# Two of 39 expert tiles of a routed feed-forward layer move into a conditional block

## The chip, the cores and the metric

The kernel runs on one core of a Trainium2 chip. Its engines are TensorE (PE, with its weight loads shown apart as PEld), VectorE (DVE), ScalarE (ACT), GpSimd (POOL) and SyncE (SP), which issues most of the DMAs. Each engine runs its own stream of instructions in order, and streams wait for each other on semaphores. The metric is the time of one execution on the device, in microseconds.

## What is computed

The reference is one decoder layer in float32 over x of 8 sequences of 512 tokens with 256 features: windowed self-attention, cross-attention to 64 context rows, and a layer of its own with attention over the 8 sequences and a mixture of 8 experts. The change concerns the experts alone:

```python
xf = y.reshape(S * B, D)                 # 4096 rows of 256
idx = jnp.argmax(xf @ Wg.T, axis=-1)     # one of 8 experts a row
out = jnp.zeros_like(xf)
for e in range(E):
    m = (idx == e)[:, None]
    h = jax.nn.relu(xf @ W1[e] + b1[e])  # 256 -> 1024
    out = out + m * (h @ W2[e] + b2[e])  # 1024 -> 256
z = layer_norm(y + out, g2, be2)         # and x + z is the result
```

Each row needs its own expert only, so how many rows an expert has depends on the data.

## The kernel before

The kernel sends each row to its expert by sorting. The last layer runs over 8 blocks of 512 rows. When a block is normalised and its experts are known (`block_end`), four indirect DMAs from POOL scatter its rows into a table in memory, `rows_d`, in which each expert has a region of its own. A row of it is 513 words: the row for the matmul, the row of the residual stream, and the number of the token.

**Tiles.** Work on the experts is cut into tiles of 128 rows of a single expert. 4096 rows make 32 full tiles, and each of 8 experts may have a last tile that isn't full, so there are at most `NT` = (4096 + 8 x 127) // 128 = 39. The kernel runs all 39, whatever the counts are.

**Three tables** say which expert and which rows a tile has. The first is made when 4 blocks are known and has the 9 full tiles that must exist by then (`NT1`); the second after 6 blocks goes up to tile 17 (`NT2`); the third, after all 8, has the remaining 22. `table` compares counts with multiples of 128: `nt` holds the tiles of each expert, `first` the sum over the experts before it. A tile past the last one used still gets an expert number (the last one's) and rows past that expert's end. For rows past the end `void` is 1, and `FAR` is added to their index, so that the gather and the scatter leave them out.

**A tile** (`expert_tile`) goes in steps. A gather by POOL brings 128 rows (L1129). SP reads the expert's number from the table into a register (L1146) and loads W1 of that expert, 1 MB (L1149), b1 (L1151) and b2, spread over the partitions (L1156). PE transposes the rows (L1167), DVE copies them out (L1169). PE makes the 1024 hidden features as 16 products (L1178), ACT and DVE take half of the relus each (L1183, L1185), PE makes 8 products with W2, which lies on the chip for all experts (L1193). DVE adds the residual (L1200) and takes mean and variance (L1203, L1204, L1206), POOL raises to the power -0.5 (L1207), DVE scales (L1209, L1210), and POOL scatters the rows to the output (L1211). At L1188 and L1189 POOL adds residual and biases.

**Order.** `expert_tile` is a generator, and each `yield` ends a step. `in_steps` runs the generators of all tiles beside each other, one step of each at a time, with tile i begun i steps late. So the first product of tile i+1 stands between the two products of tile i, and the gathers and loads run ahead. `in_order` then ties PE, DVE, ACT and POOL to the order in which instructions were written; SP's stream is placed by the framework. Six buffers take the gathered rows in turn, four the output rows (`r`, one allocation for four tiles).

Of the kernel before, what the change touches and what calls it, by code (L numbers as in the profile page):

```python
# [8 lines left out]
F32 = mybir.dt.float32  # L9
I32 = mybir.dt.int32  # L10
BF16 = mybir.dt.bfloat16
AF = mybir.ActivationFunctionType
ALU = mybir.AluOpType
# [4 lines left out]
P = 128  # L18
# [5 lines left out]
E, DF = 8, 1024  # L24
# [7 lines left out]
NGRP = S // GP  # L32
NT = (B * S + E * (P - 1)) // P
NB1, NB2 = 4, 6
NT1, NT2 = (-(-(n * NG * P - E * (P - 1)) // P) for n in (NB1, NB2))
ROW = 2 * D + 1
FAR = 1 << 20
# [2 lines left out]
PREFIX, TURN, VALUES, SMALL, SCORES, OTHER, EXPS, LOADS = range(8)  # L40
# [9 lines left out]
@contextmanager  # L50
def in_order(tc):

    traced = tc.nc.cur_bb.bb.instructions
    before = len(traced)
    yield
    et = mybir.EngineType
    last = {et.PE: None, et.DVE: None, et.Activation: None, et.Pool: None}
    for i in list(traced)[before:]:
        if i.engine in last:
            if last[i.engine] is not None:  # L60
                tc.add_manual_dep(
                    i,
                    last[i.engine].name,
                    mybir.DependencyInfo(mybir.DependencyClass.NoSync, mybir.DependencyReason.DATA),
                    reason="in_order",
                )
            last[i.engine] = i


def in_steps(works):  # L70

    step = 0
    works = sorted(works, key=lambda w: w[0])
    active, begun = [], []
    while works or active:
        while works and works[0][0] <= step:
            w = works.pop(0)
            begun.insert(0, [w[2] if len(w) > 2 else OTHER, w[1]])  # L80
            active.insert(0, begun[0])
        todo = sorted(active, key=lambda w: w[0])
        active = []
        while todo:
            w = todo.pop(0)
            rank = next(w[1], StopIteration)
            if isinstance(rank, tuple):
                w[0] = rank[1]
                todo = sorted([w] + todo, key=lambda w: w[0])
            elif rank is not StopIteration:  # L90
                w[0] = OTHER if rank is None else rank
                active.append(w)
        order = {id(w): i for i, w in enumerate(begun)}
        active.sort(key=lambda w: order[id(w)])
        step += 1
# [3 lines left out]
def decoder_kernel(ctx: ExitStack, tc: tile.TileContext, a: dict, out: bass.AP):  # L99
    nc = tc.nc  # L100
# [9 lines left out]
    rows_d = dram.tile([E * B * S, ROW], I32, name="rows_d")  # L110


    group_rows = dram_disjoint_views(rows_d, NGRP + NT)
# [95 lines left out]
    new = {}  # L209
# [4 lines left out]
    if True:  # L214
        wp = p1.enter_context(tc.tile_pool(name="wp1", bufs=1))
# [510 lines left out]
    if True:  # L726
# [277 lines left out]
        scatters = []  # L1004

        def traced():
            return nc.cur_bb.bb.instructions

        known = (4 * NB1, 4 * NB2, 4 * NBLK)
# [75 lines left out]
        def counts():  # L1085
            ps = ps_m.tile([P, E], F32, tag="m")
            nc.tensor.matmul(ps, new["ones"], seens[-1], start=True, stop=True)
            return ps

        def make_table(name, n, whole):  # L1090

            wp, taken = new["w"], new["taken"]
            rest = wp.tile([P, E], F32, name=name + "rest")
            nc.vector.scalar_tensor_tensor(rest, taken, -float(P), counts(), ALU.mult, ALU.add)
            base = wp.tile([P, E], F32, name=name + "base")
            nc.vector.scalar_tensor_tensor(
                base, taken, float(P), cst[:, C_E4 : C_E4 + E], ALU.mult, ALU.add
            )
            if whole:
                nc.vector.tensor_scalar(rest, rest, float(1 - P), None, ALU.add)  # L1100
            first, nt = table(name, rest, ALU.is_gt, n, base, not whole)
            if whole:

                take = wp.tile([P, E], F32, name=name + "take")
                nc.vector.tensor_scalar(take, first, -1.0, float(n), ALU.mult, ALU.add)
                nc.vector.scalar_tensor_tensor(take, take, 0.0, nt, ALU.max, ALU.min)
                nc.vector.tensor_tensor(taken, taken, take, ALU.add)
            yield
# [3 lines left out]
        def expert_tile(i):  # L1112
# [3 lines left out]
            k = sum(i >= n for n in at) - 1  # L1116
            (eidx, srci, void), j = tables[k], i - at[k]
            if i < 6:
# [10 lines left out]
            nc.gpsimd.indirect_dma_start(  # L1129
                out=t.bitcast(I32),  # L1130
                out_offset=None,
                in_=group_rows[NGRP + i],
                in_offset=bass.IndirectOffsetOnAxis(ap=srci[:, j : j + 1], axis=0),
                bounds_check=E * B * S - 1,
                oob_is_err=False,
            )
            gather = traced()[-1]
            for scatter in scatters[: known[k]]:
                tc.add_manual_dep(
                    gather,  # L1140
                    scatter,
                    mybir.DependencyInfo(mybir.DependencyClass.Sync, mybir.DependencyReason.DATA),
                    reason="rows",
                )
# [5 lines left out]
            b1 = small.tile([P, NFC], F32, tag="b1", name=f"b1_{i}")  # L1150
            nc.sync.dma_start(b1, a["b1"][bass.ds(e_sp, 1)].rearrange("o p c -> p (o c)"))  # L1151

            if i % 4 == 0:
                new["r"] = qsh.tile([P, 4, D], F32, tag="qT", name=f"r_{i}")
            r = new["r"][:, i % 4]
            nc.sync.dma_start(r, a["b2"][bass.ds(e_sp, 1)].to_broadcast([P, D]))  # L1156
# [35 lines left out]
            for f in range(NFC):  # L1192
# [21 lines left out]
                in_=r,  # L1214
# [11 lines left out]
            works.append((F0 + 4 * n + 15, block_end(n, 0, NG)))  # L1226
        for k, (nb, n) in enumerate(((NB1, NT1), (NB2, NT2 - NT1), (NBLK, NT - NT2))):
            works.append((F0 + 4 * nb + 16, make_table(f"t{k}", n, nb < NBLK)))
        for i in range(NT):
            works.append((F0 + 4 * NB1 + 18 + i, expert_tile(i), VALUES))  # L1230
        with in_order(tc):
            in_steps(works)


def _constants():
# [40 lines left out]
def build(nc, arrays):  # L1276
    args = {
        name: nc.dram_tensor(f"in_{name}", v.shape, mybir.dt.from_np(v.dtype), kind="ExternalInput").ap()
        for name, v in arrays.items()
    }  # L1280
    out = nc.dram_tensor("out_0", (B, S, D), F32, kind="ExternalOutput").ap()
    with tile.TileContext(nc) as tc:
        decoder_kernel(tc, args, out)
# [52 lines left out]
```

## Time and profile before

| what | us |
|---|---|
| median of 3 runs (lowest, highest) | 1179.1 (1176.48, 1179.41) |
| profiled execution | 1174.85 |
| its span, first to last instruction | 1172.9 |
| 39 gathers of tiles, first and last issue | 841.2, 1129.1 |
| first and last scatter of rows to the output, issue | 880.6, 1162.0 |

The profile is of one execution. Its span is 1.95 us shorter than the time of that execution, and that lies 4.25 us under the median of the timed runs. All times within the trace count from the start of the span. Rows of the trace name an engine, a line of the kernel, the operation and the tiles; a "q" behind an engine's name means its sequencer, which waits, branches, loads registers and issues. The costliest groups of the expert part, as the page has them (line, engine, operation, out<-in, shapes, count, then busy us, mean ns of one, and idle time of the engine just before with what ended it):

```profile
L1178 PE MATMUL hps<-tT,w 128*128 128x128 f32 x1248 | 146.1, 275 | 0.4 <-issue 0.4
...
L1193 PE MATMUL ps<-w,h 128*128 x624 | 141.0, 379 | 0.0
...
L1207 POOL TENSOR_TENSOR rs<-rs,nhalf 128x1 f32<-128x1 f32 x39 | 22.9, 588 | 77.8 <-DVE rs L1206 65.6
```

The counts are those of 39 tiles: 32 and 16 matmul instructions of each, and one power.

### The profile page before, as it was taken

To read this page: it belongs to the slowest core of one execution; us is meant where nothing else is said; L and a number is where in the kernel's file an instruction comes from. 1 tells how busy PE (TensorE), PEld (TensorE's weight loads), DVE (VectorE), ACT (ScalarE), POOL (GpSimd) and SP (SyncE) were. 2 spreads that over 40 slices of the span, in tenths; PEclk is the share of its full clock that TensorE was granted. 3 is DMA by queue.
4 is the path that set the end of the run, shared out by engine and by line. 5 is a ranking of instruction groups with operands and counts; after the bars stand their busy time and mean duration, and the time that the engine had idled before them with its cause. 6 is when DMAs were issued, how large, how long until landed. Compare 5 with 4: busy or idle time off the path is not lost.

```text
span 1172.9 us, 24541 instructions
## 1 busy us (share of the span) xinstructions
PE 1087.1 (93%) x8960; PEld 791.9 (68%) x8960; DVE 721.2 (61%) x1833; ACT 584.4 (50%) x2047; POOL 499.7 (43%) x581
## 2 busy tenths in 40 slices
PE   6798999989989989999898899999799999999995
PEld 3555656656566565665555567666588999999994
DVE  2947758588485794866743535666656765555553
ACT  2876767668686686765942265555332111111110
POOL 2242623335323353153431333545555667555553
PEclk9997999999999999999989999999999999999998
DMA  6000001010010000100001670111445968666630
GB/s 208 11 1 1 11 1 46 2 37 11 2 46 3 19 28 1 42 6 28 29 1 40 185 226 1 37 69 42 137 142 200 296 219 260 207 206 207 209 110 7
DMA packets 60742, 97.65 MB, mean 83 GB/s; under 512 B 15946, under 2 KB 43981, under 8 KB 60624
## 3 DMA queue, kind: packets, MB, share of 16 engines
q1 hardware_dynamic: 53072, 75.08, 20.4%
q0 software_dynamic: 7552, 21.02, 5.3%
q8 instruction: 72, 1.18, 0.4%
q14 instruction: 46, 0.38, 0.1%
HBM read 81.12 MB, written 17.71 MB: 84 GB/s over the span
## 4 chain that ended last, share of the span: by engine, by line
PE 71%; DVE 15%; ACT 8%; DMA 2%; POOL 2%; issue 1%; SPq 0%; POOLq 0%; DVEq 0%
PE ps L186 12%; PE ps L191 12%; PE hps L1178 12%; PE ps L1193 11%; ACT s L464 5%; DVE nm L460 2%; PE sc L417 2%; DVE s L444 2%; PE ps L180 2%; PE av L523 2%; PE ps L857 2%; PE xav L659 2%; DVE kg L377 1%; PE av L894 1%; PE pt L494 1%; DVE nm L598 1%
## 5 line engine op out<-in xcount | busy, mean ns | idle before, releaser
L464 ACT ACTIVATE s<-s,nm 128x144 f32<-128x144 f32 (+1 forms) x512 | 203.4, 406 | 12.3 <-DVE nm L460 12.3
L1183 ACT ACTIVATE h<-hps,b 128x128 f32<-128x128 f32 x156 | 44.6, 368 | 220.6 <-issue 190.3
L1178 PE MATMUL hps<-tT,w 128*128 128x128 f32 x1248 | 146.1, 275 | 0.4 <-issue 0.4
L1178 PEld LDWEIGHTS hps<-tT,w 128*128 128x128 f32 x1248 | 142.8, 192 | 1.2 <-issue 0.6
L1193 PE MATMUL ps<-w,h 128*128 x624 | 141.0, 379 | 0.0
L500 POOL TENSOR_TENSOR pc<-pT,cst 128x512 f32<-128x512 f32 x96 | 123.1, 1303 | 27.1 <-DVE pT L496 26.7
L1193 PEld LDWEIGHTS ps<-w,h 128*128 128x128 f32 x624 | 115.7, 190 | 14.1
L464 ACT ACTIVATION_READ_ACCUMULATOR s<-s,nm 128x1 f32 x512 | 100.0, 195 | 0.0
L475 POOL COPY rx<-s 128x128 f32<-128x128 f32 x48 | 14.8, 308 | 190.6 <-ACT s L464 190.6
L460 DVE TENSOR_REDUCE nm<-s 128x8 f32<-128x1152 f32 (+1 forms) x64 | 84.5, 1320 | 13.2 <-POOL s L453 9.4
L1185 DVE TENSOR_SCALAR h<-hps,b 128x128 f32<-128x128 f32 x156 | 43.9, 344 | 75.0 <-ACT h L1183 60.9
L444 DVE COPY_PREDICATED s<-upto_q,sc 128x512 f32<-128x512 int32 x96 | 65.0, 731 | 24.6 <-ACT s L443 24.5
L417 PE MATMUL sc<-kz,qT 32*128 32x512 f32 (+1 forms) x512 | 76.4, 606 | 4.0 <-DVE s L436 3.1
L159 POOL TENSOR_TENSOR rs<-rs,nhalf 128x4 f32<-128x4 f32 (+1 forms) x33 | 33.8, 1024 | 108.2 <-DVE rs L158 108.0
L494 PE MATMUL pt<-cst,s 128*128 128x128 f32 x512 | 74.0, 285 | 2.5 <-ACT pT L498 1.0
L494 PEld LDWEIGHTS pt<-cst,s 128*128 128x128 f32 x512 | 61.3, 146 | 15.6 <-issue 7.2
L443 ACT COPY s<-sc 128x512 f32<-128x512 f32 x96 | 51.6, 590 | 35.6 <-PE sc L417 35.6
L478 DVE RECIPROCAL rc<-sm 128x8 f32<-128x8 f32 x64 | 12.6, 196 | 77.6 <-ACT s L464 77.6
L186 PE MATMUL ps<-fxT,w_fwqkv 128*128 128x512 f32 x128 | 58.8, 604 | 0.0
L186 PE MATMUL ps<-xT,w_wqkv 128*128 128x512 f32 x128 | 58.3, 598 | 0.0
L883 POOL TENSOR_TENSOR fs<-fs,sm 128x512 f32<-128x512 f32 x32 | 33.4, 1044 | 56.0 <-DVE sm L882 53.7
L1207 POOL TENSOR_TENSOR rs<-rs,nhalf 128x1 f32<-128x1 f32 x39 | 22.9, 588 | 77.8 <-DVE rs L1206 65.6
(240 smaller groups left out, 2309.4 us busy)
## 6 DMA issues: line engine op xcount, KB each, us to landing
w<-in_W SPq DMA_DIRECT2D x47, 1024.0 KB
r<-in_b SPq DMA_DIRECT2D x39, 128.0 KB
xb<-in_x SPq DMA_DIRECT2D x8, 512.0 KB
y<-x2d SPq DMA_DIRECT2D x32, 128.0 KB
x2d<-xb SPq DMA_DIRECT2D x7, 512.0 KB
mi<-in_mask SPq DMA_DIRECT2D x8, 128.0 KB
mj<-in_maskT SPq DMA_DIRECT2D x8, 128.0 KB
w_wqkv<-in_wqkv SPq DMA_DIRECT2D x1, 768.0 KB
```

The lines of the kernel that those rows point to most:

```text
L186: nc.tensor.matmul(ps, w[:, k, o0 : o0 + P], xT[:, k, :], start=k == 0, stop=k == 1)
L191: nc.tensor.matmul(ps, xT[:, k, t0 : t0 + P], w[:, k, o0 : o0 + D], start=k == 0, stop=k == 1)
L417: nc.tensor.matmul(ps[j // 2][:, j % 2].rearrange("p r w k -> p r (w k)"), qT[rows[j], hf, q0 : q0 + P], kz[rows[j], hf, :, q0 + P - nw * ...
L443: nc.scalar.copy(s4, ps[jj][:, :, :, 0, :])
L444: nc.vector.copy_predicated(s4, upto_q.unsqueeze(1).unsqueeze(1).to_broadcast([P, 2, 2, P]), ps[jj][:, :, :, 1, :],)
L460: nc.vector.tensor_reduce(nm, s[:, :, :nk], AX.X, ALU.max, negate=True)
L464: nc.scalar.activation(s[:, h, :nk], s[:, h, :nk], AF.Exp, bias=nm[:, h : h + 1], accum_out=sm[:, h : h + 1],)
L494: nc.tensor.transpose(pt[:, h, :], s[:, 4 * jj + h, :P], ident)
L500: nc.gpsimd.tensor_tensor(pc[:, hs, :], pT[:, hs, :], upto_k.unsqueeze(1).to_broadcast([P, 4, P]), ALU.mult,)
L1178: nc.tensor.matmul(ps[:, f, :], w1[:, k, f * P : (f + 1) * P], tT[:, k, :], start=k == 0, stop=k == 1)
L1183: nc.scalar.activation(h[:, f, :], ps[:, f, :], AF.Relu, bias=b1[:, f : f + 1])
L1193: nc.tensor.matmul(ps, h[:, f, :], new["w2"][:, bass.ds(e_pe, 1), f, :].rearrange("p o d -> p (o d)"), start=f == 0, stop=f == NFC - 1,)
```

## The change

A constant `NTC` = 37 is added, and the pipeline holds tiles 0 to 36. Tiles 37 and 38 are written behind it, in a block that all five engines enter or jump over by a number from memory. That number, `nt_i`, is made with the third table: the sum of `first` and `nt` of the last expert, so the number of tiles that the table uses, turned into an integer. The block is entered if it is over `NTC - NT2` = 20.

```diff
+NTC = 37
...
             first, nt = table(name, rest, ALU.is_gt, n, base, not whole)
+            if not whole:
+
+                nt_all = wp.tile([P, 1], F32, name="nt_all")
+                nc.vector.tensor_tensor(nt_all, first[:, E - 1 : E], nt[:, E - 1 : E], ALU.add)
+                new["nt"] = wp.tile([P, 1], I32, name="nt_i")
+                nc.vector.tensor_copy(new["nt"], nt_all)
...
-                in_=group_rows[NGRP + i],
+                in_=group_rows[NGRP + i] if i < NTC else rows_d,
...
-            for scatter in scatters[: known[k]]:
+            for scatter in scatters[: known[k]] if i < NTC else []:
...
-            if i % 4 == 0:
+            if i % 4 == 0 or i == NTC:
                 new["r"] = qsh.tile([P, 4, D], F32, tag="qT", name=f"r_{i}")
...
-        for i in range(NT):
+        for i in range(NTC):
             works.append((F0 + 4 * NB1 + 18 + i, expert_tile(i), VALUES))
         with in_order(tc):
             in_steps(works)
+
+        with tc.If(nc.values_load(new["nt"][0:1, 0:1], min_val=0, max_val=NT) > NTC - NT2):
+            in_steps([(i, expert_tile(i), VALUES) for i in range(NTC, NT)])
```

`values_load` puts the number into a register of each of the five engines, and each engine compares and branches for itself. In the program that is built from it each engine's stream has four parts behind the pipeline: the block, a part for the other case that brings the semaphores to the values that the block would have left (with an instruction on POOL for those of the indirect DMAs), a part in which the two meet again, and the end of the program. The last steps of tile 36 (L1207, L1209, L1210, L1211) stand in the part where the two meet. In front of the compare-and-branch DVE, ACT and POOL have six semaphore waits. In the block the gathers read `rows_d` as a whole and depend on all that was written to it, where those of the pipeline have views of it and named scatters to wait for. Tile 37 takes a new allocation of output rows.

## The prediction

> **What bounds the kernel now.** I read the page's first two parts, then a table by stretches of the last 320 us, then the chain of waits at its end. In the page:
>
> ```profile
> span 1172.9 us, 24541 instructions
> ...
> PE 1087.1 (93%) x8960; PEld 791.9 (68%) x8960; DVE 721.2 (61%) x1833; ACT 584.4 (50%) x2047; POOL 499.7 (43%) x581
> ...
> PE   6798999989989989999898899999799999999995
> PEclk9997999999999999999989999999999999999998
> ```
>
> The last ten slices of PE are full, at an undiminished clock. The stretches say it in numbers (length, then busy us and count of each engine, clock, DMA share, GB/s):
>
> ```profile
> core 0: us, PE busy (x) PEld busy (x) DVE busy (x) ACT busy (x) POOL busy (x), PEclk, DMA share, GB/s
> 1050.00:1100.00 50.00, 50.00 (x346) 46.76 (x345) 24.81 (x83) 8.01 (x28) 27.82 (x35) 1.00 0.65 212
> 1100.00:1150.00 50.00, 50.00 (x346) 46.81 (x345) 24.59 (x83) 8.01 (x28) 25.78 (x32) 1.00 0.40 123
> ```
>
> From 950 us to the last matmul PE never idles, DVE and POOL are half idle, DMA has room. So the expert tiles cost what their matmuls cost. The chain's last pieces (start, length, what):
>
> ```profile
> 1130.67 3.46 PE ps L1193 x16
> 1134.13 0.22 PE pt L1167 x2
> 1134.35 3.57 PE hps L1178 x32
> 1137.92 3.46 PE ps L1193 x16
> ...
> 1148.62 3.57 PE hps L1178 x32
> 1152.19 6.92 PE ps L1193 x32
> ...
> 1160.28 0.17 DVE rs L1206
> ...
> 1160.59 0.66 POOL rs L1207
> 1161.24 0.56 issue
> 1161.80 1.28 POOLq L1282
> ```
>
> One tile is 0.22 + 3.57 + 3.46 = 7.25 us of PE. The last product ends at 1159.12; behind it stand DVE's normalisation, the power on POOL, a last scatter, and the end of the program, which hangs on one row of POOL's queue:
>
> ```profile
> L1282 POOLq DRAIN  x3: 40/107/10337, 1161.8 to 1172.7; - x3
> ```
>
> POOL drains for 10.3 us (min/median/max in ns, so the 10337 is the one that starts at 1161.80), to 1172.14; the closing barriers follow.
>
> **Is the block skipped?** The condition is "tiles of the last table over 37 - 17 = 20". Counting the reference's own argmax on these inputs gives experts of 307, 294, 269, 642, 610, 1093, 688 and 193 rows: 3+3+3+6+5+9+6+2 = 37 tiles, 17 of them in the first two tables, so exactly 20. The trace agrees. Here are the moments at which the scatters of tiles 35 to 38 move data:
>
> ```profile
> 1145.90:1146.60 0.70, 0.70 (x5) 0.62 (x4) 0.17 (x1) 0.50 (x2) 0.70 (x2) 1.00 0.53 187
> 1153.10:1153.80 0.70, 0.70 (x5) 0.61 (x4) 0.34 (x2) 0.32 (x2) 0.70 (x2) 1.00 0.27 96
> 1160.10:1160.80 0.70, 0.00 (x0) 0.00 (x0) 0.67 (x3) 0.00 (x0) 0.21 (x1) 1.00 0.04 1
> 1163.50:1164.20 0.70, 0.00 (x0) 0.00 (x0) 0.00 (x0) 0.00 (x0) 0.00 (x0) 0.50 0.04 1
> ```
>
> 187 GB/s for a full tile, half of it for tile 36 (193 - 128 = 65 rows), nothing for tiles 37 and 38: all their rows lie past the bound. They cost PE time and yield nothing.
>
> **Removed.** Two tiles: on PE 2 x 7.25 = **14.50 us**, all on the path, since the stretch from 1144.62 to 1159.12 holds 14.48 us of PE work. With them go on SP two loads of W1 (1 MB each), of b1 and b2 and two index loads; on POOL two gathers, two scatters and six small operations; on DVE and ACT the relus and normalisation. None of it ended a wait of PE here, so it brings nothing more. The end of the pipeline keeps its form: in the built order tile 36 takes the place of tile 38 (first product of 36, second product of 35, second product of 36), with 3.46 us of PE between the relus of 36 and their use, as before.
>
> **Added at the last table.** Two DVE operations on 128x1. The nearest rows are the 128x1 casts and adds of L1160 and L1206, 0.154 us each; with the wait between them some 0.4 us near 958 us. DVE has 50 us less 30.6 of work in that stretch and PE runs from tiles loaded ahead, so I take 0. Without this cover it is 0.4 once.
>
> **Added: the condition's value.** Each engine loads it into a register. SP's stands where the index loads of tiles 37 and 38 stood, behind the table that it waits for: nothing new to wait for, and one load of the same kind fewer. On the others the load stands behind the last work of the main part. Its price is that of the loads that PE's queue does already:
>
> ```profile
> L1171 PEldq TENSOR_LOAD <-t2eidx x22: 295/300/325, 992.8 to 1144.8; - x22
> ```
>
> **Moved, and this is the price.** The built order shows that the last third of tile 36 (L1209 and L1210 on DVE, the power L1207 and the scatter L1211 on POOL) now stands *behind* the branch. PE, ACT and SP branch too, but nothing is queued behind theirs except the closing barrier, and SP stood finished at 1164.87 with POOL's drain open to 1172.14: 7 us of cover.
>
> DVE, behind its L1206: six semaphore waits on things long done (0.06 apart in SP's closing rows) 0.36, load 0.30[...], one wait and one semaphore update 0.06[...]: 0.88 us. Before, L1209 ran beside the power and ended (1160.82) before it (1161.24). Now it starts at about 1161.2 in the old clock, ends at 1161.65, and L1210 starts some **0.4 us** later than its 1161.28. POOL passes its own branch after the scatter of tile 35, done issuing (1159.64) 0.8 us before the power is due: some 1.2 us of the same kind of steps, so the power starts 0.3 late, inside the 0.4. [...]
>
> [...] In this trace the fetches of instructions are single packets of 8 KB (16 KB for PE) that take 0.3 to 1.5 us each[...]. The block jumped over has 32 instructions on DVE and 19 on POOL[...]. [...] at its worst it is one fetch on each of the two, side by side: a packet of up to 1.3 us plus a round trip like that of the last scatter (issue 1162.05, its landing seen at 1164.26: 2.2 us), at most 3.5 us. I take 0.4, nearer to nothing[...].
>
> POOL's skip path also holds an instruction that books the four indirect DMAs that were not issued. One of its kind, in another mode, took 31 ns at the start. Above, it could behave as the drain does and wait out the scatter before it: 1172.14 less 1163.08 is 9.1 us. I take the row of its own kind, 0. Below nothing it can't go.
>
> Last, the final scatter is now tile 36's, with 65 real rows: its packets took 0.42 us against 0.19 for an empty one. 0.2 at most, if the drain waits for them.
>
> **Sum:** -14.5 + 0.4 + 0.4 + 0.2 = **-13.5 us**. The profiled execution took 1174.85 (span 1172.9 and 1.95 around it) and would take 1161.4. The three timed runs lie higher, with their median at 1179.1; I take off the same: **1165.6**.
>
> **Rivals.**
> - *The branch misses its instructions* (chance 0.09). 3.5 in place of 0.4: 1168.7. For it, POOL and DVE both jump at the one place where the end hangs on them[...].
> - *The booking instruction waits like a drain* (0.05). 9.1 more: 1174.7, still 4.4 under before. For it, the 10.3 us drain, which nothing else in the trace explains: SP saw the last DMA land 7.9 us before its end. Against it, 31 ns of the other one.
> - *The end doesn't move* (0.03): the drain is a backlog of POOL's software for indirect DMAs and not a tail behind the last one. Then it ends where it did: 1179. Against it, each of the last five scatters moves its data 1.6 us after its issue (1137.16 to 1138.77, and so on to 1162.05 to 1163.67), so nothing piles up.
> - *The block is entered* (0.04), slower. The point is one tile more than 20. Then the gathers of 37 and 38, so far issued two tiles ahead, start behind POOL's branch: 1144.6 + 1.7 for scatter and branch + 2.2 to land + 1.0 for transposing and copying = 1149.5, then both tiles' products, 14.06, end at 1163.6 instead of 1159.12; tile 36's own last third (0.48, 0.66, scatter) comes after: +4.5 + 2.5, some 1186. Against it, the count and the rows of 1 GB/s.
>
> **How the numbers follow.** The forecast has 0.79, with a range of its own from 1160.3 (the profiled execution less 14.5) to 1167.5. The three rivals that stay at or under before have 0.17, the slower one 0.04. The range of 8 in 10 takes in the missed fetch and the spread of the runs: 1160.3 to 1171. Under about 0.3%, 3.5 us, a measurement can't tell a change from none. Faster: forecast, missed fetch and most of the waiting booking, 0.91. Same: the rest of that and the end that doesn't move, 0.05. Slower 0.04.
>
> **What would show it.** Right: 37 tiles in the trace, PE ending near 1144.6, no gap in it before; L1210 of tile 36 less than 1 us later behind the last product than the 2.16 us of now; POOL's drain again near 10 us. Wrong: a hole of over 2 us on DVE or POOL between L1206 and L1209 (missed fetch), or between the booking and the power (drain); a drain that ends at 1172 in spite of an earlier scatter; 39 tiles.

## The result and the profile after

Measured beside each other, the kernel before took 1177.89 us (median of 4, 1176.48 to 1179.41) and the changed one **1164.14 us** (median of 4, 1163.32 to 1165.42): ratio 0.9884, interval [0.9865, 0.9903], so 13.75 us less. The forecast was 13.5 less, to 1165.6 from the 1179.1 that stood before it.

The page after shows that two tiles are gone. PE's part of the 40 slices is full to the last but one, as before:

```profile
span 1163.0 us, 24277 instructions
...
PE 1075.7 (92%) x8860; PEld 777.9 (67%) x8860; DVE 713.9 (61%) x1811; ACT 582.0 (50%) x2039; POOL 491.7 (42%) x571
...
PE   6888999998999989999899899999979999999994
PEclk9897999999999999999989899999989999999998
```

8860 matmuls where 8960 were: 2 tiles of 16 + 32 + 2 instructions. The end by stretches, first of the kernel before and then of the changed one. Each first row begins with the same matmul, the 8601st of PE's order, and ends with the last; the second row is the tail behind it:

```profile
1105.41:1159.10 53.69, 53.69 (x362) 49.79 (x360) 26.73 (x88) 8.01 (x28) 26.56 (x34) 1.00 0.31 99
1159.10:1172.90 13.80, 0.00 (x1) 0.00 (x0) 2.06 (x6) 0.00 (x0) 2.23 (x3) 0.61 0.00 0
```

```profile
1108.65:1147.84 39.19, 39.19 (x262) 36.21 (x260) 19.48 (x64) 5.72 (x20) 18.42 (x24) 1.00 0.22 73
1147.84:1163.00 15.16, 0.00 (x0) 0.00 (x0) 2.16 (x6) 0.00 (x0) 2.12 (x3) 0.64 0.04 13
```

Three things are to be read here.

- **PE.** 53.69 less 39.19 is 14.50 us, with PE busy through both stretches: exactly two tiles of 7.25, and nothing late in front of them.
- **The start.** The 8601st matmul comes 3.24 us *later* in the changed kernel's profiled execution. The code up to there is the same but for the two small operations at the third table, and the lag is there before it, by 880 us. PE's clock was halved for 40.9 us of the first 600 against 34.1 (the rows of PEclk differ in their second slice, 8 against 9); 6.8 us more at half the clock lose up to 3.4. It is an affair of these two executions, and it is why their spans differ by 9.9 only, where the medians differ by 13.75.
- **The tail** got longer by 1.33 us (13.85 to 15.18, counted from the unrounded end of the last matmul).

So -14.50 + 3.24 + 1.33 = -9.9 for the two spans, and -13.2 without the late start, beside -13.75 of the medians.

Where the 1.33 comes from is seen in the timeline behind the last product (start, length, what, idle before it and its releaser):

```profile
1149.01 0.15 DVE L1213 TENSOR_SCALAR rs<-mv 128x1 f32<-128x1 f32 x1
1150.54 0.48 DVE L1216 SCALAR_TENSOR_TENSOR r<-r,mv,bc_g 128x256 f32<-128x256 f32 x1 [1.37 <-DVEq L1241]
1151.06 0.56 POOL L1214 TENSOR_TENSOR rs<-rs,nhalf 128x1 f32<-128x1 f32 x1 [2.68 <-DVE r L1216]
1151.65 0.49 DVE L1217 SCALAR_TENSOR_TENSOR r<-r,rs,tb 128x256 f32<-128x256 f32 x1 [0.62 <-POOL rs L1214]
1152.42 1.03 POOL L1218 DMA_INDIRECT out<-r,to  x1 [0.81 <-DVE r L1217]
```

and in the instructions of L1241, the line of the condition (ns min/median/max, first and last start), with POOL's drain below:

```profile
L1241 DVEq EVENT_SEMAPHORE  x7: 21/50/50, 1149.0 to 1150.4; - x7
L1241 POOLq TENSOR_LOAD <-nt_i x1: 499/499/499, 1147.6 to 1147.6; - x1
L1241 POOLq COMPARE_BRANCH  x1: 45/45/45, 1148.2 to 1148.2; - x1
L1241 POOLq INC_SWDGE_SEM  x1: 2301/2301/2301, 1148.6 to 1148.6; - x1
L1241 DVEq TENSOR_LOAD <-nt_i x1: 540/540/540, 1149.6 to 1149.6; - x1
L1241 DVEq COMPARE_BRANCH  x1: 72/72/72, 1150.2 to 1150.2; - x1
```

```profile
L1292 POOLq DRAIN  x3: 40/113/10010, 1152.2 to 1162.7; - x3
```

DVE finished rs at 1149.16 and stood for 1.37 us at waits, load and branch. POOL, beside it, was busy from 1148.59 to 1150.89 with one instruction, `INC_SWDGE_SEM`, the booking of the indirect DMAs that were not issued. Only then could it raise to the power, and DVE's last scaling waited for that. The timeline names DVE's L1216 as releaser of the power. That is the event that came last, but the power doesn't use its result; POOL's own booking held it up to 1150.89. The power starts 0.17 us behind the end of the booking, and so it does in the repeat and with 38 tiles; in the last of these it starts before L1216 has ended (1156.72, and 1156.27 + 0.48). The chain of waits goes further astray. Its first piece is

```profile
1110.59 40.20 DMA tb<-rows_d,t2srci
```

that is, a gather of 40 us as the cause of the end. No gather took that long; PE had read the last of them long before. The next piece is POOL's L1241 at 1150.78, so by the semaphores from which the chain is inferred it steps from the end of the booking (1150.89) back to a real gather.

### The profile page after: what moved, and what is told of

The parts are those of the page before. It is cut to its first block, busy times and chain, and to the rows that moved or that the text cites. A ratio compares the mean times of both kernels' runs of the same rounds, so it can differ in the third digit from the quotient of the medians.

```text
span 1163.0 us, 24277 instructions
## 1 busy us (share of the span) xinstructions
PE 1075.7 (92%) x8860; PEld 777.9 (67%) x8860; DVE 713.9 (61%) x1811; ACT 582.0 (50%) x2039; POOL 491.7 (42%) x571
## 4 chain that ended last, share of the span: by engine, by line
PE 64%; DVE 16%; ACT 7%; DMA 6%; POOL 2%; issue 2%; SPq 0%; POOLq 0%; DVEq 0%
PE ps L187 12%; PE ps L192 12%; PE hps L1185 9%; PE ps L1200 8%; ACT s L465 5%; DMA tb<-rows_d,t2srci 3%; DVE nm L461 3%; DVE s L445 3%; PE sc L418 2%; PE xav L660 2%; PE ps L181 2%; PE av L524 2%; PE ps L858 2%; DVE kg L378 2%; PE av L895 1%
## 5 line engine op out<-in xcount | busy, mean ns | idle before, releaser
L1185 PE MATMUL hps<-tT,w 128*128 128x128 f32 x1184 | 138.6, 275 | 0.1
L1185 PEld LDWEIGHTS hps<-tT,w 128*128 128x128 f32 x1184 | 135.5, 192 | 0.8 <-issue 0.4
L1200 PE MATMUL ps<-w,h 128*128 x592 | 133.7, 379 | 0.0
L1200 PEld LDWEIGHTS ps<-w,h 128*128 128x128 f32 x592 | 109.7, 190 | 13.4
L427 PEld LDWEIGHTS pq<-kg,qT 128*128 128x128 f32 x96 | 14.7, 193 | 58.7 <-ACT pT L499 19.2
```

What stands on the lines that cost most here:

```text
L1185: nc.tensor.matmul(ps[:, f, :], w1[:, k, f * P : (f + 1) * P], tT[:, k, :], start=k == 0, stop=k == 1)
L1200: nc.tensor.matmul(ps, h[:, f, :], new["w2"][:, bass.ds(e_pe, 1), f, :].rearrange("p o d -> p (o d)"), start=f == 0, stop=f == NFC - 1,)
```

## The experiments

Two questions stood open: what made the tail 1.33 us longer, and what POOL's drain of 10 us is, which no step of mine explained and which stands in both kernels. Each ratio is taken to runs of the kernel before on the same chip.

| kernel | median us | ratio to before, interval | tail us |
|---|---|---|---|
| changed kernel again | 1165.65 | 0.9884 [0.9858, 0.991] | 15.16 |
| no block | 1163.86 | 0.9859 [0.9832, 0.9885] | 13.52 |
| last tile ahead of the branch | 1166.88 | 0.9894 [0.9868, 0.9921] | 16.08 |
| block entered | 1189.89 | 1.0083 [1.0055, 1.011] | 16.3 |
| 38 tiles and a block of one | 1170.62, one run | | 15.28 |
| no block, no last scatter | 1159.41, one run | | 11.61 |
| a drain in every tile | 1174.85 | 0.9978 [0.9969, 0.9987] | 7.87 |
| the same, last tile ahead of the branch | 1172.72 | 0.9962 [0.9949, 0.9976] | 6.81 |
| drains from tile 22, last tile ahead | 1155.91 | 0.981 [0.9795, 0.9826] | 6.81 |
| one drain in tile 30, last tile ahead | 1155.95 | 0.9811 [0.9796, 0.9825] | 6.80 |
| before with drains from tile 22 | 1169.72 | 0.9939 [0.9926, 0.9953] | 6.57 |

The kernels before were at 1178.9 beside the first four, 1177.13 beside the next four, 1177.47 beside the last three.

### The changed kernel again

No edit: the reference for the three that ran beside it.

> The changed kernel once more, on the same chip as the three beside it. From its profile: 37 tiles, the last matmul 14.5 us earlier than before once the clock's slow stretches before 870 us are taken out, and from the last matmul to the end of the span 15.1 us (before: 13.8). POOL's instruction that books the skipped DMAs takes 2.3 us again. Time about 1164, ratio 0.988. If instead the 2.3 us was an accident of one execution, the tail is near 14.5.

The ratio came out the same and so did the tail (15.16 us, the booking at 2.29 us). The tail's length is the same in both; what moves by some us is the part in front of 900 us, and not by the clock alone: here the 8601st matmul came at 1109.42, 4.0 later than in the kernel before, with the clock halved for as long as there (61.4 us up to 900). Why, no run shows. From the 8601st matmul to the last it is 39.19 us again. So in what follows the tail is read from the profile, to some 0.1 us, and the medians only where their intervals lie apart.

### No block

```diff
-        with tc.If(nc.values_load(new["nt"][0:1, 0:1], min_val=0, max_val=NT) > NTC - NT2):
-            in_steps([(i, expert_tile(i), VALUES) for i in range(NTC, NT)])
```

> Leaves out tiles 37 and 38 and the conditional block altogether. If the block costs what the profile of the changed kernel shows (L1217 of the last tile starts 3.8 us behind the last matmul and not 2.2), the tail from the last matmul to the end of the span is 13.4 to 13.9 us and the time 1.3 to 1.6 us under the changed kernel's, about 1162.7. If the block costs more elsewhere (six waits, loads, an order of SP or DVE in the pipeline), it is lower still, and the last matmul comes earlier too. If it costs nothing and the tail differs for another reason (the 65 real rows of the last scatter), the tail stays 15.1.

Without the block the tail is 13.52 us, and the last scaling starts 2.17 us behind the last matmul, as before the change. So everything that the branch costs is 15.16 - 13.52 = 1.64 us. (By the medians it is 1.8, but the intervals of the two ratios overlap.) The tail is also 0.33 *shorter* than that of the kernel before, although its last scatter moves 65 rows and not none:

```profile
L1289 POOLq DRAIN  x3: 40/107/10010, 1152.9 to 1163.4; - x3
```

The drain ended 8.73 us behind the end of the scatter's instruction, and 9.06 in the kernel before. The scatter with real rows made it no longer.

### The last tile ahead of the branch

```diff
         with in_order(tc):
             in_steps(works)
+            used = nc.values_load(new["nt"][0:1, 0:1], min_val=0, max_val=NT)

-        with tc.If(nc.values_load(new["nt"][0:1, 0:1], min_val=0, max_val=NT) > NTC - NT2):
+        with tc.If(used > NTC - NT2):
```

Written in order, the register loads come behind tile 36's last steps and take them ahead of the branch.

> The register loads of the condition are tied behind the last instruction of DVE and POOL, so the last steps of tile 36 stand in front of the branch. If the cost of the block is its place ahead of these steps, L1217 starts 2.2 us behind the last matmul again, the 2.3 us of booking and the branch fall into POOL's drain, and the tail is 13.4 to 13.9 us, time about 1162.7. Rival: the drain begins to count when it is issued and lasts 10 us whatever was before it; then branch and booking, some 3.3 us, are added behind the last scatter, the tail is about 17 us, and the time 1166.

The last scaling was early again (2.18 us), so the delay did come from what stood in front of it. But the tail was 16.08 us, longer than with the branch in front. POOL's rows show the reason, the booking and then the drain:

```profile
L1242 POOLq INC_SWDGE_SEM  x1: 2315/2315/2315, 1152.5 to 1152.5; - x1
```

```profile
L1293 POOLq DRAIN  x3: 40/107/8723, 1154.9 to 1164.1; - x3
```

The booking now stands between scatter and drain, and the drain, begun 2.3 us later, still takes 8.72 us. If the drain waited for the scatter to land, the booking would have hidden 2.3 us of it. The two add up, as POOL's own work in its own queue would. In the changed kernel all but some 0.5 us of the booking is hidden beside DVE's work and branch; here nothing of it is.

### The block entered

```diff
-        ...  > NTC - NT2):
+        ...  > NTC - NT2 - 1):
```

The block's two tiles run, though all their rows lie past the end.

> The threshold is one lower, so that the block is entered with these counts, and runs the two empty tiles. By the working of the prediction the gathers start behind POOL's branch, the two tiles' products take 14.1 us of PE behind a hole of some 5 us, and the last steps of tile 36 come after: some 7 us over the kernel before, about 1185. Rival: the loads of W1 and the gathers are quick enough that the hole is 2 us or less, then it ends 3 to 4 us over before, about 1181. If the body of the block has to be fetched, the hole is 8 us or more, about 1188.

It is slower than the kernel before, by 9.8 us by the ratio (0.83% of 1178.9) and 11.0 by the medians. PE at the block, in the timeline:

```profile
1141.98 7.07 PE L1200 MATMUL ps<-w,h 128*128 x32
1152.54 0.41 PE L1174 MATMUL pt<-cst,tb 128*128 128x128 f32 x2 [3.49 <-DMA tb<-rows_d,t2srci]
1154.64 0.69 PE L1174 MATMUL pt<-cst,tb 128*128 128x128 f32 x2 [1.70 <-DMA tb<-rows_d,t2srci]
1155.12 9.47 PE L1185 MATMUL hps<-tT,w 128*128 128x128 f32 x64
1164.43 7.07 PE L1200 MATMUL ps<-w,h 128*128 x32
```

From 1149.05 to 1155.12 PE has no product to do, 6.1 us: the gathers begin behind the branch, and in PE's order the transposes of both tiles stand ahead of the first product, so that it waits for the second gather too. And the two tiles then take 16.4 us (1155.12 to 1171.50) instead of 14.06, which I had not seen. By stretches:

```profile
1149.05:1155.10 6.05, 0.87 (x4) 0.66 (x5) 1.93 (x7) 0.00 (x0) 3.78 (x5) 0.81 0.34 83
1155.10:1164.40 9.30, 9.30 (x66) 9.30 (x65) 1.55 (x5) 1.14 (x4) 1.70 (x3) 0.76 0.26 102
1164.40:1171.50 7.10, 7.10 (x34) 5.92 (x32) 3.19 (x10) 1.14 (x4) 1.11 (x2) 1.00 0.00 1
```

PE has no gap behind 1155.12, so it waits for nothing there: its clock is down, to 0.76 of the full one in the middle row. It was halved from 1152.8 to 1159.6. Matmuls start 0.213 us apart up to there and 0.112 behind it; the 21 that fell into the slow part cost 2.1 of the 2.3 us. Whether the hole brings this about no run tested. (SP stood for 7.1 us in front of b2 of tile 37, for scatters from output rows that the new allocation takes, and W1 of tile 38 was issued behind that; as PE shows no gap, it made nothing later.)

### How much is booked, and what is drained

Two kernels, each timed once, for the booking and for the drain. The first keeps 38 tiles in the pipeline, so that two and not four indirect DMAs are skipped; the second has no block and leaves out the last scatter.

```diff
-NTC = 37
+NTC = 38
```

> NTC = 38: one empty tile more in the pipeline, one in the skipped block, so POOL has two skipped indirect DMAs to book and not four. If the booking has a price for each DMA, it takes about 1.2 us; then DVE's branch decides and L1217 starts some 3.2 us behind the last matmul, not 3.8. If its price is fixed, or is a wait, 2.3 us again. The last matmul stands 7.25 us later than in the changed kernel against the matmuls of the tiles before. The drain at the end has 108 indirect DMAs behind it: if its length goes with their number (110: 9.06 us behind the end of the last one, 106: 8.73), it is 8.90.

```diff
-            nc.gpsimd.indirect_dma_start(
+            if i != NTC - 1:
+                nc.gpsimd.indirect_dma_start(
...
```

> As e1, without the block, and the scatter of tile 36 is left out, so that 65 rows of the output aren't written. The drain now stands directly behind the power L1214, which ends 2.14 us behind the last matmul; the last indirect DMA (tile 35) ended 1.6 us before that. If the drain is a work of its own, 0.082 us for each of the 105 indirect DMAs so far, it ends 8.65 us behind the power, 10.8 behind the last matmul. If it is a lag behind the last indirect DMA, it ends 8.7 us behind that one's end, 9.3 behind the last matmul. If it waits for the last DMA to be written, the same.

```profile
L1241 POOLq INC_SWDGE_SEM  x1: 2334/2334/2334, 1154.2 to 1154.2; - x1
```

```profile
L1292 POOLq DRAIN  x3: 40/113/10172, 1157.8 to 1168.6; - x3
```

```profile
L1290 POOLq DRAIN  x3: 40/107/9363, 1147.5 to 1157.4; - x3
```

The first two rows are of the kernel with 38 tiles, the third of the one without the last scatter. Half as many DMAs booked, and the booking is not shorter but 0.03 us longer. And without any scatter in front of it the drain still runs for 9.36 us, to 8.67 us behind the end of the power, POOL's last work. So the last scatter doesn't set its end. (A drain's row can begin while work of POOL stands queued ahead of it, as in the changed kernel, at 1152.18 with the scatter's from 1152.42 to 1153.46, so it is measured from the end of POOL's last work.) What does go with it is the number of indirect DMAs that the program had issued; the last two rows are from kernels further below, where a drain stands earlier:

| kernel | indirect DMAs since the start | drain's end behind POOL's last work, us | per DMA, us |
|---|---|---|---|
| before, block entered | 110 | 9.06 | 0.0824 |
| 38 tiles | 108 | 8.90 | 0.0824 |
| changed, no block, last tile ahead | 106 | 8.73 to 8.75 | 0.0824 to 0.0826 |
| no last scatter | 105 | 8.67 | 0.0825 |
| one drain in tile 30, that drain | 95 | 7.97 | 0.084 |
| drains from tile 22, the first of them (changed, before) | 79 | 6.70, 6.55 | 0.085, 0.083 |

The four DMAs that are booked and not issued don't count: with and without the block the drain is the same. Every one of these DMAs moves 128 rows or leaves them out, so whether the price goes by the DMA or by the row isn't shown. The booking follows the same number: 2.30 us behind 105 issued, 2.315 behind 106, 2.334 behind 107. That made a forecast: a drain in between should empty the account, and both should become short.

### A drain in every tile

```diff
             nc.gpsimd.tensor_tensor(t[:, D : 2 * D], t[:, D : 2 * D], new["be2"], ALU.add)
+            nc.gpsimd.drain()
```

> The changed kernel with one drain of POOL more in each tile, behind L1196, where POOL stands idle for 2.6 us of each 7.25. If a drain's length goes with the indirect DMAs issued since the drain before, each costs 0.3 us in that hole (the first one 2 to 3 us, for the scatters of the blocks), the one at the end has two left, 0.3 us, and SP's closing waits for the last landing set the end: tail 15.2 - 8.4 + some 0.9 = 7 to 8.5 us, time about 1157. If the end's drain has a fixed length, or waits for something else than these, the tail stays 15 us. If the drains in the middle wait for the DMAs in flight to land, POOL loses 2 us or more in each tile, gathers come later, and PE shows holes.

> e2 and e7 together: the last steps of tile 36 in front of the branch, and a drain in each tile. If e2 was late because booking (2.3 us) and a drain of 8.7 us follow each other on POOL, then with a short drain the tail is last scatter at 2.95 + 1.03, branch and booking to 6.5, drain 0.3, closing 0.8: about 7.6 us, 0.5 to 1 under e7, time about 1156. Rival: each drain costs PE something in the pipeline; then the last matmul comes later than in the changed kernel by more than 1 us against its clock, and the gain is eaten.

(The second has this edit and that of the last tile ahead of the branch.) At the end of the program it went as forecast; of the first kernel:

```profile
L1242 POOLq INC_SWDGE_SEM  x1: 211/211/211, 1165.6 to 1165.6; - x1
...
L1197 POOLq DRAIN  x37: 2642/5777/9050, 864.4 to 1157.3; - x37
```

The booking fell from 2.30 to 0.21 us, in the same place, with a scatter just in front of it; so it doesn't wait for scatters. The tail fell to 7.87 us, and to 6.81 with the last tile ahead. The drain at the end took 0.96 us in the second:

```profile
L1294 POOLq DRAIN  x3: 46/107/963, 1168.8 to 1170.9; - x3
```

The 1.06 between the two tails is in the main DVE's waits, load and branch (the last scaling starts 3.29 and 2.18 us behind the last matmul), since the booking is over before DVE has branched.

But the time moved little, 0.2 and 0.4%, and the row of L1197 says why: a drain *between* tiles takes 2.6 to 9.1 us, far over the 0.08 to 0.33 that the one to four DMAs since the drain before would make by the count. The traces show what sets its end. In all four kernels with drains in several tiles, each drain from 1016 us on but the first ends 0.4 to 1.3 us behind the last packet of an indirect DMA (0.4 to 2.3 before 1016 us), and so do the short ones at the end. So such a drain goes with the landing of the transfers in flight; the count rules where many DMAs stand behind the drain. POOL's gathers and scatters written behind it come later for it: the single drain further below, of 11.1 us, brought a gather 5.4 us nearer to its use. By stretches, with drains and then without (the changed kernel):

```profile
900.00:1016.00 116.00, 106.80 (x720) 95.87 (x717) 63.17 (x223) 18.07 (x59) 66.04 (x77) 0.97 0.60 203
1016.00:1060.00 44.00, 44.00 (x304) 41.10 (x304) 23.94 (x77) 6.84 (x24) 30.48 (x35) 1.00 0.59 193
```

```profile
900.00:1016.00 116.00, 115.86 (x827) 107.92 (x827) 70.29 (x251) 19.36 (x65) 77.34 (x91) 1.00 0.72 239
1016.00:1060.00 44.00, 44.00 (x307) 41.22 (x306) 21.99 (x73) 6.87 (x24) 24.67 (x32) 1.00 0.60 197
```

While attention still shares the engines, PE gets 720 matmuls done where it did 827, being idle for 9 us of the 116 and at a lower clock, 0.97. From 1016 us on, drains or not, PE is full. So a drain costs PE nothing there.

### Drains only where PE has cover

```diff
             nc.gpsimd.tensor_tensor(t[:, D : 2 * D], t[:, D : 2 * D], new["be2"], ALU.add)
+            if i >= 22:
+                nc.gpsimd.drain()
```

with the last tile ahead of the branch; then the same with `i == 30`, so a single drain; and `i >= 22` in the kernel before, without any block.

> e8 with drains in tiles 22 to 36 alone. In e7 and e8 the last matmul came some 17 us late against the clock, and all of that arose before 1016 us, where POOL still works for the blocks; from there on PE kept 7.25 us a tile in spite of drains of 3.5 to 8.5 us. So with late drains PE should stand as in the changed kernel, the first drain (some 70 indirect DMAs behind it) take 6 to 9 us without harm, the booking take 0.2 us, the drain at the end 1 us, and the tail 6.8 us and not 15.2: time about 1156, ratio 0.981. Rival: the first long drain holds up a gather by more than the pipeline has in hand, and PE has a hole of 2 to 6 us at about 1040: then 1158 to 1162.

> e2 with a single drain, in tile 30 (some 88 indirect DMAs behind it, 7 to 9 us). If length goes with the number, 16 or so are left at the end: 1.3 us more or less hidden behind the closing waits of SP, booking 0.5 us, tail 7 to 8 us, time about 1156.5. If it needs a drain in each tile, the tail is above 10. If POOL can't spare 8 us at once, PE has a hole near 1095 us.

> The kernel before, 39 tiles, with drains in tiles 22 to 38. If the drain at the end is the indirect DMAs' own affair and has nothing to do with the conditional block, this falls by the same 6.5 to 7 us as e10 against e1 (tail from 13.8 to 6.5 to 7), time about 1171, and e10 lies 14 to 15 us under it. If the gain of e10 were a matter of the booking and the branch, this stays near 1178.

Both versions of the changed kernel are faster than either kernel: 1155.91 and 1155.95 us, at ratios of 0.981 whose intervals lie apart from the changed kernel's 0.9884. The one with a single drain, its booking, the mid drain and the end:

```profile
L1244 POOLq INC_SWDGE_SEM  x1: 415/415/415, 1153.8 to 1153.8; - x1
...
L1198 POOLq DRAIN  x1: 11111/11111/11111, 1098.6 to 1098.6; - x1
...
L1295 POOLq DRAIN  x3: 46/107/1168, 1154.3 to 1156.2; - x3
```

and PE around that drain:

```profile
1098.00:1110.00 12.00, 12.00 (x80) 11.09 (x80) 3.53 (x12) 2.28 (x8) 3.60 (x5) 1.00 0.77 273
```

POOL drains for 11.1 us in tile 30 (7.97 of them behind the work that was queued ahead of the drain), and PE goes on without a hole. A gather is issued 12.1 us ahead of its transposes; the one that this drain held up still came 6.7 us ahead, and two tiles later it is 11.3 again. 8 us that nothing can cover at the end have become 11 that are covered. In the kernel before the same drains bring 0.6%: 7.8 us by the medians, 7.3 by the tail (13.85 to 6.57). So this gain has nothing to do with the block; the two tiles and the drain add up (1155.91 lies 13.8 under 1169.72).

## Why the prediction was right, and where its numbers were off

- **The bound and the part removed: right.** 14.50 us of PE by the sum, 14.50 measured; no idle came in front, and nothing more was gained elsewhere. DVE, ACT, SP and POOL had been no bound there.
- **The block is skipped: right**; with the threshold one lower it is entered, so the number was 20 exactly. The price of that rival was near: 1186 said, 1189.9 measured. The tail's +2.5 came out. Missing was PE's clock behind the hole (16.4 us of products in place of 14.06), and the hole was 6.1 us where my sum made it 4.9, since it counted one gather and not both.
- **Branches of PE, ACT and SP: covered**, as said. PE's compare-and-branch took 258 ns, four to six times that of the others, at 1144.2, where it kept nothing waiting.
- **DVE's branch: the step was right, a term was short.** I had 0.88 us from the end of rs to the first scaling, where 1.37 were measured, and 0.4 on the path. The six waits came 0.1 us apart and not 0.06, and the load took 0.54 and not PE's 0.30; the branch itself took 0.07. Of the 0.88, 0.72 rested on rows of the trace before; the other 0.16, for the branch and a jump, was not shown by any. DVE's steps alone make the last scaling 1.1 us late and not 0.4, as the kernel with drains in every tile shows, where it starts 3.29 us behind the last matmul and not 2.17.
- **No fetch was missed.** Between the end of the branch and the first instruction at its target lay 0.16 us on DVE and 0.13 on POOL, over 32 and 19 instructions. The last instruction fetch of the trace begins at 1144.41 and takes 0.93, ahead of POOL's branch (1148.16) and DVE's (1150.20). The 0.4 set aside for a fetch was my own guess, with no row behind it, and had nothing to pay for. A longer jump no run tested.
- **The booking at 0: the step that failed.** I took it from a row of 31 ns of the same instruction in another mode. It took 2.30 us. POOL's start of it before the end of DVE's rs hid most, and it made the last scaling later by another 0.5. In all that is 1.63, from 2.18 to 3.81, where 0.8 was forecast with the fetch; the sign that I had named, less than 1 us later, didn't show. The rival "the booking waits like a drain" was wrong in its cause, for it waits for no scatter, and in its 9.1 us; what the two share is the count.
- **The last scatter at +0.2: wrong in sign.** The drain got 0.33 shorter, four indirect DMAs fewer at 0.082. I had set the drain down as a tail behind the last scatter, and turned down "a backlog of POOL's software" because that drain would end at a fixed time. It goes by count (0.082 us each) and follows POOL's last work: it moves with the scatter, and yet it grows with the count as a backlog would.

Summed up, the tail was +1.33 where I had +1.0: errors of +0.8 and -0.5 half cancelled, and that was luck. That the total met the difference of the medians within 0.3 us rests on the 14.50; the profile's own sum, -13.2, misses it by 0.6. The 1165.6 lies 1.5 over the 1164.14 since the kernel before stood at 1177.89 beside it and not at 1179.1.

## What to carry to other kernels

The branches of PE, ACT and SP (0.26, 0.05 and 0.05 us, with loads of 0.31, 0.66 and 0.27) kept nothing waiting here, because nothing urgent stood behind them. So look in the built order at what each engine has queued behind its branch, and write the last steps of the last work ahead of the branch if what follows the branch has cover. Here that order alone made the tail 0.9 us longer, and with the drains in place 1.06 shorter. A time at the very end that no transfer explains deserves a kernel of its own: here one drain, put where the bounding engine has work laid in, was worth 8 us without touching the mathematics. And where a profile names a cause that the code can't need (a gather of 40 us, a releaser whose result isn't read), ask which instruction of the waiting engine's own queue stood in between.

## What the runs showed of the hardware

- **POOL's drain costs by count.** Behind many indirect DMAs it ended 0.082 to 0.085 us for each of those issued since the previous drain behind the end of POOL's last work: 6.55 and 6.70 us behind 79, 7.97 behind 95, 8.67 behind 105, 9.06 behind 110. Empty and full transfers counted alike. Behind one to four it ended 0.4 to 2.3 us behind the last packet in flight instead, and at the end of the program, behind 2 to 11, 1.0 to 1.5 us behind POOL's last work. Behind 24, with transfers in flight (the first drain of the two kernels with one in every tile), it took 2.9 to 3.1, more than the 2.0 of the count. What it does in that time the traces don't show.
- **The booking of skipped indirect DMAs** costs by the same count and not by what it books: 2.30 us behind 105, 0.415 behind 11, 0.24 behind 2, about 0.20 + 0.020 for each.
- **Steps of a conditional.** Register load 0.50 to 0.69 us on POOL, DVE and ACT, 0.16 to 0.31 on SP and PE; compare and branch 0.04 to 0.07 us, on PE 0.08 to 0.39.
- **PE's clock at a hole.** With the block entered, the clock was halved for 6.8 us, beginning 3.8 us into a hole of 6.1, and the products behind the hole took 2.3 us longer. That the hole is the cause was not tested by itself.
